# Attention on one core: a step's value products issued ahead of the next pair's score products

## The chip, the cores and the metric

The kernel runs on one core of a Trainium2 chip. The core has a matrix engine (PE; its weight loads are shown as an engine of their own, PEld), a vector engine (DVE), a scalar engine (ACT), a general engine (POOL) and a queue that issues transfers (SP). Each engine works through its own instructions in the order written, and the engines wait for one another through semaphores. The metric is the device time of one execution of the whole program, in microseconds (us).

## The reference

The program is two transformer layers on `x` of 8 batches by 256 rows by 512 columns: a convolution with a gated product, a ternary feed-forward, an attention over `ctx_2048`, and a mixture of experts. The change is in the attention, which is, cut to what is computed:

```python
q = rms_norm(x @ Wq + bq, gq).reshape(b, -1, n, d)          # n = 16 heads of d = 32
k_img = rms_norm(ctx_img @ Wk_img + bk_img, gk_img).reshape(b, -1, n, d)
v_img = (ctx_img @ Wv_img + bv_img).reshape(b, -1, n, d)
scores = jnp.einsum('bqnd,bknd->bnqk', q, k) * scale
probs = jax.nn.softmax(scores, axis=-1)
img_x = jnp.einsum('bnqk,bknd->bqnd', probs, v)
out = (txt_x + img_x).reshape(b, -1, n * d)
return out @ Wo + bo                                        # added to x
```

The image part of the context is its first 257 rows. A batch has 256, so the text part is empty, and each batch attends its 256 queries to its 256 context rows. `x` is layer-normalised before, and the result is layer-normalised again for the experts that follow.

## The kernel before, in words

The attention is one loop (from L1326) over 64 steps plus four iterations that drain the pipeline. A batch has eight steps, k = n % 8: two halves i of 128 query rows, in each two pairs of head groups `cp`, in each two sub-steps p. One step handles four heads for 128 queries, that is 128 x 1024 scores. All engines but SP are held to the order in which the loop writes its instructions (`in_order`, L58), so the source order is the order on PE, DVE, ACT and POOL.

In iteration n these pieces are written, in this order, each for the step that is due:

- `normalise` (L1240) of step n-1: DVE takes the reciprocal `rden` of the row sums, POOL multiplies the probabilities `pr` by it.
- on odd n, `exps` (L1231) of step n: four exponentials on ACT with their row sums.
- on even n, `scores` (L1209) of steps n and n+1: eight products on PE, each on 32 of the array's rows, into two `sc` tiles; then `largest` (L1224) of step n on DVE, which gives `mx`.
- `turn` (L1248) of step n-2: PE transposes `pr` in two groups of four into two `pt` tiles of the tag "tr"; the first is copied to SBUF by DVE (L1262), the second by ACT (L1260). The copies are named `pts`.
- on even n, `largest` of step n+1 and `exps` of step n.
- for k below 6, a piece of the next batch: `middle`, `value` and `end` (L924 to L988) project its k, q and v (eight matmuls of 512 columns, written by `project`, L862), add biases, normalise, and transpose the results. The last batch has no next one, and in the batch before it the value projections come at k = 5 and k = 7 (L1359).
- near the end, normalised rows `dxn` for the experts, which PE transposes into `dxT` (also of the tag "tr") and DVE copies to `xT` (L1312).
- on even n from 4, `values` (L1265) of step n-3: 16 products on PE, each into 32 of the array's columns, which need the four `pts` tiles of steps n-4 and n-3. Their sum `o` is copied by ACT to `oT` (L1278).
- for the last step of each half, `project_out` (L1280): four c-chunks of the output projection into `fo`, which DVE adds to the rows `xs` (L1287) and POOL completes with the bias (L1288). With the halves 0 and 1 of batch 6 it is put off to iterations 56 and 61 (L1318).

The PSUM pool `psC` has two buffers for each tag: "sc" for scores, "tr" for every transposed tile, "mm" for projections, `o` and `fo` alike. A tile takes the buffer of the tile before last of the same tag, and has to wait until that one has been read. In the records every fp32 product of PE shows as two loads and two matmuls.

```python
if 3 <= n < len(steps) + 3 and steps[n - 3].p:
    steps[n - 3].values(steps[n - 4])                 # L1385, L1386
```

Of the kernel before, what the change touches and what calls it, by code (L numbers as in the profile page):

```python
# [78 lines left out]
def tile_kernel(ctx: ExitStack, tc: tile.TileContext, a: dict, out: bass.AP):  # L79
# [795 lines left out]
    def gate_tile(name):  # L875

        pool = experts if len(taken) % 5 == 4 else gates
        taken.append(name)
        return pool.tile([P, DC, TB], F32, tag="gu", bufs=1 if pool is experts else 4, name=name)
# [4 lines left out]
    def gate_weights(names, e, name):  # L884
        gu = gate_tile(f"{name}_gu").rearrange("p c (k f) -> p c k f", k=2)
        for k in range(2):
            nc.sync.dma_start(gu[:, :, k, :], of_expert(names[k], e).rearrange("(c p) f -> p c f", p=P))
        return gu
# [304 lines left out]
    with tc.tile_pool(name="att", bufs=2) as ap_, tc.tile_pool(  # L1193
# [86 lines left out]
        def project_out(b, i, oT):  # L1280
            T = xs[:, i, b, :]
            fo = pc.tile([P, D], F32, tag="mm", name=f"fo{b}{i}")
            for c in range(DC):
                nc.tensor.matmul(  # L1284
                    fo, lhsT=oT[:, c, :], rhs=wsb["Wo"][:, c, :], start=(c == 0), stop=(c == DC - 1)
                )
            nc.vector.tensor_tensor(T, T, fo, ALU.add)  # L1287
            nc.gpsimd.tensor_tensor(T, T, wsb["bo"], ALU.add)  # L1288
# [23 lines left out]
        def turn_in(t, xn):  # L1312
            ps = transposed(pc, xn, f"dxT{t}", "tr")
            nc.vector.tensor_copy(xTs[t // 4][:, :, t % 4 * P : (t % 4 + 1) * P], ps)  # L1314
# [6 lines left out]
        steps, later = [], {}  # L1321
# [4 lines left out]
        for n in range(len(steps) + 4):  # L1326
            coming = None
            k = n % 8
            if n < len(steps):
                if k == 0 and 0 < steps[n][0] < B - 1:  # L1330
                    batches[-1].load()
                if n % 2 == 0:
                    for j in (n, n + 1):
                        steps[j] = Step(batches[steps[j][0]], *steps[j][1:])
                if k < 6 and steps[n].b + 1 < B:
                    coming = batches[steps[n].b + 1]
            if 0 < n <= len(steps):
                steps[n - 1].normalise()
            if coming:
                coming.begin(k)  # L1340
            if n < len(steps) and n % 2:
                steps[n].exps()
            if k == 7 and n > 8:
                finished.root.log()
            if n < len(steps) and n % 2 == 0:
                steps[n].scores(steps[n + 1])
                steps[n].largest()
            if 2 <= n < len(steps) + 2:
                steps[n - 2].turn()
            if n < len(steps) and n % 2 == 0:  # L1350
                steps[n + 1].largest()
                steps[n].exps()
            if coming:
                coming.middle(k)
                if k > 3 and coming.b < B - 1:
                    coming.value(k - 4)
                coming.end(k)
            at = n - (len(steps) - 8)
            if at in (-3, -1):  # L1359
                batches[-1].value((at + 3) // 2)  # L1360
            if at == 1:

                nmr = stat.tile([P, 8], F32, tag="nmr8", bufs=1, name="d_nmr")
                nc.vector.scalar_tensor_tensor(
                    nmr, dmv[:, 0:8, 0], -1.0, dr[:, 0:8], ALU.mult, ALU.mult
                )
            if at == 2:
                for tb in range(2):
                    xTs.append(gate_tile(f"xT{tb}"))
                gu0 = gate_weights(("sg", "sw1"), 0, "s0")  # L1370
            if at in NORMED:
                for t in NORMED[at]:
                    xn = ap_.tile([P, D], F32, tag="xn", bufs=2, name=f"dxn{t}")
                    nc.scalar.activation(
                        xn, xs[:, t % 2, t // 2, :], AF.Identity, bias=nmr[:, t : t + 1], scale=dr[:, t : t + 1]
                    )
                    done_norms[t] = xn
            if k == 7 and n + 9 < len(steps):
                batches.append(Batch((n + 9) // 8, (ap_, ap_), pc))
                batches[-1].moments()  # L1380
            if k == 6 and n > 8:
                finished = Norm((n - 14) // 8)
            elif k == 7 and n > 8:
                finished.factor()
            if 3 <= n < len(steps) + 3 and steps[n - 3].p:  # L1385
                steps[n - 3].values(steps[n - 4])  # L1386
            if n >= 4 and steps[n - 4].cp and steps[n - 4].p:
                s = steps[n - 4]
                if (s.b, s.i) in put_off:
                    later[len(steps) - 8 + put_off[s.b, s.i]] = s  # L1390
                else:
                    project_out(s.b, s.i, s.oT)
            if n in later:
                project_out(later[n].b, later[n].i, later[n].oT)

            for t in NORMED.get(at - 1, ()):
                turn_in(t, done_norms[t])
# [561 lines left out]
```

## Time and profile before

| what | us |
|---|---|
| median of three runs | 1156.17 |
| lowest and highest of them | 1151.67 and 1158.35 |
| the profiled execution's own time | 1151.6 |
| its span, first to last record | 1149.8 |
| first score product of the attention | 380.5 |
| last output projection's add begins | 748.8 |
| one middle batch | 47 |

The profiled execution lies at the low end of the runs, 4.6 us under their median, and 1.8 us of its time lie outside its span. Its granted PE clock is full in all slices.

A line of a timeline is the start in us, the duration in us, the engine, the source line, the operation, the output and inputs, the shapes and the count. What stands in square brackets is the idle time of the engine just before, and what ended it. "issue" means that nothing is shown that it waited for. A line of the stages is the stretch, its length, each engine's busy time with its number of instructions, the clock, the share of the DMA engines and GB/s.

### The profile page before, as it was taken

The page shows a single profiled execution, that of the slowest core. Times are in us where ns is not written, and L with a number is a line of the kernel's source. Part 1 is how long each engine was busy: PE and PEld are TensorE (multiplying, and loading weights), DVE is VectorE, ACT ScalarE, POOL GpSimd, SP SyncE. Part 2 cuts the span into 40 slices and gives each one's busy share as a digit, 9 for nine tenths or more (in the row PEclk, how much of TensorE's full clock was granted, in tenths as well). Part 3 has the DMA queues.
Part 4 walks back from the last instruction along what each step waited for, and adds up shares of the span by engine and source line. Part 5 has one row for each costly group of instructions (what it writes and reads, how often), then busy time and mean ns, then how long its engine had stood idle before and what let it go on. Part 6 is the DMA issues. An engine that isn't in the chain of part 4 may idle for free.

```text
span 1149.8 us, 16488 instructions
## 1 busy us (share of the span) xinstructions
PE 1094.3 (95%) x5866; PEld 658.8 (57%) x5885; DVE 683.6 (59%) x1507; ACT 520.8 (45%) x1173; POOL 440.2 (38%) x501
## 2 busy tenths in 40 slices
PE   4999998899999999999999998899999999999997
PEld 3777775454545555555655555554466766675443
DVE  5998999798866565765656756637612222222452
ACT  4437645798884555656556565531011121111000
POOL 5788887244331243433333434313770000000650
PEclk9999999999999999999999999999999999999999
DMA  7424520699500100000000010052668999997571
GB/s 272 154 74 150 153 76 20 236 305 291 141 1 19 37 1 4 16 19 1 20 20 1 2 38 1 1 194 102 240 202 269 306 338 330 301 314 240 155 248 40
DMA packets 122780, 153.26 MB, mean 133 GB/s; under 512 B 7481, under 2 KB 81273, under 8 KB 122178
## 3 DMA queue, kind: packets, MB, share of 16 engines
q1 hardware_dynamic: 108608, 116.49, 32.1%
q10 hardware_dynamic: 8962, 18.85, 4.6%
q0 software_dynamic: 5120, 16.78, 4.4%
q8 instruction: 49, 0.80, 0.3%
q14 instruction: 41, 0.34, 0.1%
HBM read 107.66 MB, written 44.43 MB: 132 GB/s over the span
## 4 chain that ended last, share of the span: by engine, by line
PE 76%; DVE 14%; POOL 4%; issue 2%; ACT 1%; DMA 1%; SPq 1%; POOLq 0%; DVEq 0%; ACTq 0%
PE r_h L1689 10%; PE gu L1504 9%; PE y L693 5%; PE k_mm L865 5%; PE fo L1284 5%; PE v_mm L865 5%; PE r_po L1705 5%; PE q_mm L865 5%; PE po L1526 5%; PE pt L1255 5%; PE f_op L473 2%; PE sc L1219 2%; PE f_hp L399 2%; PE o L1274 2%; PE o_h L1746 2%
## 5 line engine op out<-in xcount | busy, mean ns | idle before, releaser
L1244 POOL TENSOR_TENSOR pr<-pr,rden 128x1024 f32<-128x1024 f32 x64 | 121.1, 1893 | 155.8 <-DVE rden L1242 140.6
L693 PE MATMUL y<-kv,tp 128*128 128x288 f32 x640 | 161.7, 408 | 5.2 <-DVE wl L716 5.0
L693 PEld LDWEIGHTS y<-kv,tp 128*128 128x128 f32 x640 | 119.0, 190 | 42.5 <-PE y L693 10.1
L1235 ACT ACTIVATE pr<-sc,mx 128x256 f32<-128x256 f32 x256 | 118.3, 483 | 8.1 <-DVE mx L1227 6.9
L1842 POOL DMA_INDIRECT yg<-yd,slot x32 | 33.1, 1035 | 224.4 <-PE gu L1504 206.3
L1689 PE MATMUL r_h<-r_xT,r_gu 128*128 128x256 f32 x512 | 113.7, 380 | 1.5 <-ACT r_xT L1676 1.5
L1689 PEld LDWEIGHTS r_h<-r_xT,r_gu 128*128 128x128 f32 x512 | 96.8, 190 | 22.4 <-issue 8.0
L1227 DVE TENSOR_REDUCE mx<-sc 128x4 f32<-128x1024 f32 x64 | 77.5, 1212 | 4.5 <-PE sc L1219 4.5
L1255 PE MATMUL pt<-ident,pr 128*128 128x128 f32 x512 | 70.6, 279 | 7.5 <-DVE xT L1314 3.5
L1696 DVE SCALAR_TENSOR_TENSOR r_y<-r_h,eb,r_ge 128x256 f32<-128x256 f32 x32 | 15.5, 483 | 97.7 <-PE r_h L1689 94.4
L1260 ACT COPY pts<-pt 128x512 f32<-128x512 f32 x64 | 37.8, 590 | 73.2 <-PE pt L1255 73.2
L1255 PEld LDWEIGHTS pt<-ident,pr 128*128 128x128 f32 x512 | 55.0, 140 | 26.1 <-issue 14.6
L1695 ACT ACTIVATE r_ge<-r_h,gb 128x256 f32<-128x256 f32 x32 | 15.1, 473 | 109.0 <-PE r_h L1689 109.0
L399 PE MATMUL f_hp<-w1q,f_xq 128*128 128x512 bf16 x245 | 59.4, 379 | 5.3 <-ACT f_xq L376 4.5
L631 POOL TENSOR_TENSOR kv<-kx 128x2048 f32<-128x2048 f32 x16 | 57.6, 3601 | 12.9 <-ACT kx L617 12.9
L865 PE MATMUL k_mm<-Wk_sb,cx 128*128 128x512 f32 x128 | 58.1, 598 | 0.0
L865 PE MATMUL v_mm<-Wv_sb,cx 128*128 128x512 f32 x128 | 57.7, 593 | 0.0
L1705 PE MATMUL r_po<-r_w,r_y 128*128 128x512 f32 x128 | 57.7, 593 | 0.0
L1284 PE MATMUL fo<-Wo_sb,oT 128*128 128x512 f32 x128 | 57.7, 593 | 0.0
L865 PE MATMUL q_mm<-Wq_sb,xT 128*128 128x512 f32 x128 | 57.6, 593 | 0.0
L1516 ACT ACTIVATE ge<-gu,gb 128x512 f32<-128x512 f32 x16 | 11.0, 687 | 102.6 <-PE gu L1504 93.8
L473 PE MATMUL f_op<-w2q,f_hq 128*128 128x512 bf16 x249 | 57.0, 379 | 0.4
(486 smaller groups left out, 2104.5 us busy)
## 6 DMA issues: line engine op xcount, KB each, us to landing
xd<-blank SPq DMA_DIRECT2D x1, 15360.0 KB, 59.2
tp<-kpd SPq DMA_DIRECT2D x32, 256.0 KB, 3.3
r_gu<-in_rg SPq DMA_DIRECT2D x16, 512.0 KB, 6.6
r_gu<-in_rw SPq DMA_DIRECT2D x16, 512.0 KB, 6.8
r_w<-in_rw SPq DMA_DIRECT2D x16, 512.0 KB, 6.8
r_xr<-xd SPq DMA_DIRECT2D x16, 512.0 KB, 6.9
yd<-r_yo ACTq DMA_DIRECT2D x32, 256.0 KB, 5.7
yd<-blank SPq DMA_DIRECT2D x1, 6144.0 KB, 77.9
```

The source lines that it names most:

```text
L399: nc.tensor.matmul(dst, lhsT=self.xq[:, i, c, :], rhs=w1q[:, c, cols], start=(c == 0), stop=False)
L473: nc.tensor.matmul(op, lhsT=self.hq[i][:, c, :], rhs=w2q[:, c, :], start=(c == 0), stop=(c == FC - 1))
L693: nc.tensor.matmul(y[:, ll, :, 0:PAIRS], lhsT=tp[:, dl : dl + P], rhs=view(kv, (m0 * G + hh) * PAIRS, [[G * PAIRS, B], [1, PAIRS]]), start ...
L865: nc.tensor.matmul(t, lhsT=lT[:, c, i * P : (i + 1) * P], rhs=w[:, c, :], start=(c == 0), stop=(c == DC - 1),)
L1227: nc.vector.tensor_reduce(self.mx, self.sc.rearrange("p r c k -> p (r c) k"), AX.X, ALU.max, negate=True)
L1235: nc.scalar.activation(self.pr[:, h // 2, h % 2, :], self.sc[:, h // 2, h % 2, :], AF.Exp, bias=self.mx[:, h : h + 1], accum_out=self.den[ ...
L1244: nc.gpsimd.tensor_tensor(flat, flat, rden.unsqueeze(2).to_broadcast([P, 4, S]), ALU.mult)
L1255: nc.tensor.transpose(pt[:, cc, k, :], self.pr[:, rr, cc, k * P : (k + 1) * P], ident)
L1284: nc.tensor.matmul(fo, lhsT=oT[:, c, :], rhs=wsb["Wo"][:, c, :], start=(c == 0), stop=(c == DC - 1))
L1504: nc.tensor.matmul(ps, lhsT=w[0][:, c, k, f * P : (f + 1) * P], rhs=xTs[tb][:, c, :], start=(c == 0), stop=(c == DC - 1),)
L1689: nc.tensor.matmul(ps, lhsT=self.w[0][:, c, k, f * P : (f + 1) * P], rhs=self.xT[:, c, 0:n], start=(c == 0), stop=(c == DC - 1),)
L1705: nc.tensor.matmul(po, lhsT=self.y[:, f, i * P : (i + 1) * P], rhs=self.w[1][:, f, :], start=(f == 0), stop=(f == EC - 1),)
```

## The change

The two lines that write `values` are moved up in the iteration: behind `exps` and the logarithm of the norm, ahead of the scores. Nothing is added or taken away.

```diff
@@ -1342,6 +1342,9 @@
                 steps[n].exps()
             if k == 7 and n > 8:
                 finished.root.log()
+            if 3 <= n < len(steps) + 3 and steps[n - 3].p:
+
+                steps[n - 3].values(steps[n - 4])
             if n < len(steps) and n % 2 == 0:
                 steps[n].scores(steps[n + 1])
                 steps[n].largest()
@@ -1382,8 +1385,6 @@
                 finished = Norm((n - 14) // 8)
             elif k == 7 and n > 8:
                 finished.factor()
-            if 3 <= n < len(steps) + 3 and steps[n - 3].p:
-                steps[n - 3].values(steps[n - 4])
             if n >= 4 and steps[n - 4].cp and steps[n - 4].p:
                 s = steps[n - 4]
                 if (s.b, s.i) in put_off:
```

`values` runs on even n only, since n-3 has to be a step with p = 1. So PE's order in an even iteration goes from scores, transposes, next batch's piece, values to values, scores, transposes, next batch's piece. On ACT the copy to `oT` goes from the iteration's end to a place ahead of the copy of `pts` and of the exponentials.

## The prediction

> **What bounds the kernel now.** I read the page first, then the stages of the attention, then the timeline of one middle batch, its weight loads alone, and the last batch.
>
> ```profile
> PE 1094.3 (95%) x5866; PEld 658.8 (57%) x5885; DVE 683.6 (59%) x1507; ACT 520.8 (45%) x1173; POOL 440.2 (38%) x501
> ...
> PE 76%; DVE 14%; POOL 4%; issue 2%; ACT 1%; DMA 1%; SPq 1%; POOLq 0%; DVEq 0%; ACTq 0%
> ```
>
> PE is the bound, and most of the chain that ended last is PE. The attention divides in two, as the stages show:
>
> ```profile
> core 0: us, PE busy (x) PEld busy (x) DVE busy (x) ACT busy (x) POOL busy (x), PEclk, DMA share, GB/s
> ...
> 568.00:615.00 47.00, 46.86 (x346) 27.06 (x345) 30.18 (x70) 27.59 (x96) 17.60 (x10) 1.00 0.04 12
> ...
> 701.00:749.00 48.00, 41.00 (x401) 26.03 (x400) 28.89 (x56) 28.63 (x91) 21.40 (x14) 1.00 0.01 1
> ```
>
> In a middle batch PE is never idle for long: only what PE's queue itself takes, and any new wait, can move the time. In the last batch, which has no next batch to project, PE idles 7 us and waits in turn for POOL, ACT and DVE; there the order of the small blocks decides.
>
> The timeline of iterations 6 and 7 of a middle batch has the place that matters most:
>
> ```profile
> 553.09 0.74 PEld L1219 LDWEIGHTS sc<-kT_T,qT_T 32*128 32x128 f32 x16 [0.17 <-issue]
> ...
> 554.16 0.86 PEld L1255 LDWEIGHTS pt<-ident,pr 128*128 128x128 f32 x8 [0.33 <-issue]
> ...
> 554.27 1.22 DVE L1227 TENSOR_REDUCE mx<-sc 128x4 f32<-128x1024 f32 x1
> ...
> 555.19 0.81 PEld L1274 LDWEIGHTS o<-pts,v 128*32 128x32 f32 x32 [0.17 <-issue]
> ...
> 555.30 0.59 ACT L1260 COPY pts<-pt 128x512 f32<-128x512 f32 x1 [4.72 <-PE pt L1255]
> 555.41 0.68 DVE L1262 COPY pts<-pt 128x512 f32<-128x512 f32 x1
> ...
> 556.41 0.85 PEld L1255 LDWEIGHTS pt<-ident,pr 128*128 128x128 f32 x8 [0.41 <-POOL pr L1244]
> ```
>
> Here values stand between two transposes of probabilities (554.16 and 556.41), with no projection near. While PE does values, DVE takes the maximum and copies the first `pt`, ACT copies the second: both "tr" buffers are free (556.09, 555.89) before the next transposes.
>
> **The change part by part.** It moves 32 calls. Each issues 16 products on PE (32 loads and 32 matmuls in the records) and one `oT` copy on ACT (0.37 us); nothing on DVE, POOL or SP, and no DMA. PE's calls are moved past eight score products, eight transposes and the next batch's piece, ACT's copy past the `pts` copy, the exponentials and the squares. So PE's work is unchanged; what changes is gaps between blocks, buffers, and when the scores come.
>
> *Gaps.* From load to load, values take 1.01 us (531.43 to 532.44), scores 1.07, transposes 0.82, and a projection with the transposes behind it 4.31, read where the loop has no values yet:
>
> ```profile
> 391.44 0.30 PEld L865 LDWEIGHTS q_mm<-Wq_sb,xT 128*128 128x128 f32 x2
> ...
> 394.55 0.14 PEld L1255 LDWEIGHTS pt<-ident,pr 128*128 128x128 f32 x1 [0.24 <-issue]
> 394.98 0.80 PEld L1255 LDWEIGHTS pt<-ident,pr 128*128 128x128 f32 x7 [0.29 <-issue]
> 395.75 0.30 PEld L865 LDWEIGHTS q_mm<-Wq_sb,xT 128*128 128x128 f32 x2
> ```
>
> The transposes' first load goes ahead of the projection's end; that of values does not. The timeline blames a DVE result for it:
>
> ```profile
> 531.43 0.81 PEld L1274 LDWEIGHTS o<-pts,v 128*32 128x32 f32 x32 [0.76 <-DVE k_r L143]
> ```
>
> Yet scores behind a projection have the same 0.76 us put down to issue (541.21), so this is the projection draining, and no wait that the move removes. In iterations 2 and 3 of a batch the stretch from scores to the second q projection is now 525.89 to 533.27 = 7.38; in the new order it is 1.01 + 1.07 + 0.82 + 4.31 = 7.21, a gain of 0.17. In 4 and 5 it is 7.37 (541.21 to 548.58), a gain of 0.16. In 0 and 1 it is 7.57 (560.87 to 568.44), a gain of 0.36, because a buffer wait goes too:
>
> ```profile
> 568.44 0.30 PEld L865 LDWEIGHTS k_mm<-Wk_sb,cx 128*128 128x128 f32 x2 [0.17 <-DVE k_pre L962]
> ```
>
> The "mm" buffers alternate; with `o` now ahead of the first k projection, the second takes `o`'s buffer, which ACT frees early, and no longer that of the first. Sum: 6 x 0.36 + 6 x 0.17 + 6 x 0.16 = 4.1 us less.
>
> The gap from values to scores is in no row. By what goes out, values leave 0.20 ahead of anything, transposes 0.17, scores 0.33, a projection 0.76. Bounds: 0.17 and 0.76. I take 0.20, since the gap follows what goes out wherever I can compare, and keep 0.33 for the range.
>
> [...]
>
> *The stall between iterations 6 and 7.* In the new order: values 553.09, scores 554.10, transposes 555.17. The maximum follows the scores by 1.18 (541.21 to 542.39), so it runs at 555.28, the `pts` copy of DVE 1.14 behind it at 556.42 to 557.10, and the next transposes, which need that buffer, load 0.06 later at 557.16: 0.75 later than 556.41. POOL's `pr` (to 556.35) is then not the last. Batches 0 to 5: 6 x 0.75 = 4.5 us more.
>
> Is anything else late? DVE is busy without a pause from 554.13 to 569, so it stays 1.01 late until iteration 1, where it waits 3.13 us (572.18); all of it ends there. On the way ACT's copy of the second `pts` of step 5 moves from 560.23 to 560.98 and ends at 561.54, and values of iteration 0 come at 561.62: met by 0.08, and each 0.1 us by which it fails costs 0.6 over six batches. The k projection of iteration 0 now takes `fo`'s buffer, free at 563.96, and comes at 564.5. POOL ends `pr` of step 7 at 567.16, ahead of the transposes at 567.7. I charge nothing for the later scores in iterations 0, 2 and 4 (0.5 to 1.0 us): the 3.6 us projections hide the maximum and the copies. Without that cover it would be another 0.75 each, 18 x 0.75 = 13.5. The `oT` copy costs nothing either: ACT waits there for transposes anyhow (4.72 at 555.30, 3.34 at 543.42); uncovered it is 32 x 0.37 = 12.
>
> [...]
>
> *Batches 6 and 7.* Batch 6 has no projection in iteration 4, so the stall comes there too: its transposes, at 686.39 for POOL, come at 686.41, but DVE's and ACT's later copies are 1.01 and 0.76 late, and the transposes behind them (688.76, 689.59) are held by just these: +0.77 at 689.98. In 6 and 7, +0.95 (696.73 becomes 698.45): +1.72 at the start of batch 7. There I follow the same rules from block to block. These rows of before carry it:
>
> ```profile
> 717.45 0.64 ACT L1260 COPY pts<-pt 128x512 f32<-128x512 f32 x1
> ...
> 717.67 0.73 PEld L1219 LDWEIGHTS sc<-kT_T,qT_T 32*128 32x128 f32 x12 [1.34 <-ACT pr L1235]
> ...
> 722.20 0.42 PEld L1255 LDWEIGHTS pt<-ident,pr 128*128 128x128 f32 x4 [0.58 <-DVE xT L1314]
> ```
>
> ```profile
> 732.82 0.42 PEld L1255 LDWEIGHTS pt<-ident,pr 128*128 128x128 f32 x4 [2.13 <-DVE xT L1314]
> ```
>
> Iteration 58: values wait for the copies of step 55 and push the scores, but the transposes wait for POOL as before: 711.97 becomes 713.48, +1.51. Iteration 60: values need the `pts` of step 57, which ACT copies behind the exponentials at 717.45; with scores behind values, the transposes go from 718.73 to 721.45, +2.72. Iteration 61: DVE's maxima are later, `xT` with them, and 722.20 becomes 725.27, +3.07. Iteration 63: scores behind values cost 1.0 again, and 732.82 becomes 736.89, +4.07. In 64 and 65 a little returns: the last transposes' second half, 741.94 before, comes 3.9 late, and so does all behind it. Batches 6 (from iteration 4) and 7: 3.9 us more. Between +1.7 (batch 7 costs nothing more) and +6 (each of its four scores a full 1.07 late).
>
> Sum: -4.1 + 4.5 + 3.9 = +4.3 us. The profiled execution's 1151.6 becomes 1155.9; against the median of 1156.17, 4.6 above it, 1160.5.
>
> **The rivals.** The forecast is a small loss, below the 0.5% (5.8 us) that a measurement of this kernel can tell from no change.
>
> *Slower: the switch from values to scores costs more.* They split the array in different ways, and no row shows one behind the other. At scores' 0.33 the 30 places give 30 x 0.13 = 3.9 more: +8.2, 1164.4. At 0.76 it is +21, 1177. It decides from 0.25. For it: no row excludes it. Against it: the gap follows what goes out.
>
> *Nothing.* If the last batch gives its 2.2 us back in the routing that follows, or the stall is 0.4, the sum is +2: 1158. The chain of waits, PE in most of its pieces from there on, speaks against it.
>
> *Faster.* If neither stall nor tail appears, the gaps remain: -4.1, 1152.1. It would need `pts` copied ahead of the maximum, which the held order forbids.
>
> **How the numbers follow.** The forecast 0.55, its own range +1 to +8 (a quarter of it beyond 5.8); the switch 0.25; nothing 0.14; faster 0.06. From these: slower 0.55 x 0.25 + 0.25 x 0.9 = 0.36, faster 0.04 (only with the runs' own spread), same 0.60. The range goes from 1155, below the case of nothing by the spread of medians, to 1167, above the switch at 0.33.
>
> **What would show it.** Right: in a middle batch, the second transposes of iteration 7 wait 0.9 to 1.2 us for DVE's `pts`, the wait on `k_pre` is gone, batches take 47.0 to 47.1, and the attention's end moves by about 4. Wrong: a gap above 0.25 ahead of scores behind values; values of iteration 0 waiting for ACT's copy; transposes in iterations 1, 3 or 5 waiting for anything.

## The result, and the profile after

The median went from 1152.82 us (8 runs, 1151.36 to 1158.35) to 1161.97 us (8 runs, 1160.89 to 1164.80): a ratio of 1.0074, 95% interval 1.0054 to 1.0093. That is slower, by more than the 0.5% that tells from no change, where the forecast had put no change first. 1161.97 lies inside the range, 1.5 above the 1160.5.

The times of before fall into groups, for a reason shown below, and 1152.82 lies in the gap between two of them (four of its runs up to 1151.79, four from 1153.84). A median jumps there, so for sums I use means. With the later comparisons there are 58 runs of before, mean 1154.4 (median 1155.13); the 8 runs after have the mean 1162.4. So the change costs 8.0 us, where +4.3 was forecast.

The page's first and fourth parts for the kernel after:

```profile
PE 1096.1 (95%) x5885; PEld 662.6 (57%) x5885; DVE 684.0 (59%) x1507; ACT 522.0 (45%) x1173; POOL 440.5 (38%) x501
...
PE 77%; DVE 15%; POOL 3%; issue 2%; DMA 1%; ACT 1%; SPq 1%; ACTq 0%; DVEq 0%; POOLq 0%
```

PE is the bound as before. The profiled execution took 1160.89 us with a span of 1159.2, against 1151.6 and 1149.8: 9.4 more span. To find where they arise I lined up the first PE load of the same blocks in both traces. The attention starts 0.25 us earlier in the trace after (380.27 against 380.52), and the table has what is added from there to each place. The last column is the prediction's own path, and the column before it is of an experiment told below, in which PE's clock stayed full through the attention.

| block | before | after, later by | same order, clock kept full | predicted |
|---|---|---|---|---|
| iteration 52, first block | 682.34 | +1.18 | +1.18 | +0.36 |
| iteration 54 | 693.61 | +4.75 | +1.93 | +1.13 |
| iteration 56 | 701.19 | +5.76 | +2.93 | +2.08 |
| iteration 60, transposes | 718.73 | +6.79 | +3.96 | +3.08 |
| iteration 63, second half | 732.82 | +8.04 | +5.21 | +4.43 |
| last output projection | 745.07 | +9.64 | +5.12 | +4.3 |

Six batches together bring only 1.18. The large jumps are +3.57 between iterations 52 and 54 and +1.60 behind iteration 63. In the column with the full clock the path is the predicted one, 0.8 higher, all of which is there by iteration 52. The last line counts what lies between the two starts; the span, which grew by 9.4, has the 0.25 in it. That output projection before, after, and in the experiment with the full clock, whose attention starts at 382.57:

```profile
745.07 0.30 PEld L1284 LDWEIGHTS fo<-Wo_sb,oT 128*128 128x128 f32 x2
...
754.46 0.30 PEld L1284 LDWEIGHTS fo<-Wo_sb,oT 128*128 128x128 f32 x2
...
752.23 0.30 PEld L1286 LDWEIGHTS fo<-Wo_sb,oT 128*128 128x128 f32 x2
```

**The middle batch.** The timeline of iterations 6 and 7 after, from one batch's seam to the next:

```profile
553.36 0.81 PEld L1274 LDWEIGHTS o<-pts,v 128*32 128x32 f32 x32 [0.17 <-issue]
554.37 0.74 PEld L1219 LDWEIGHTS sc<-kT_T,qT_T 32*128 32x128 f32 x16 [0.20 <-issue]
554.74 1.89 POOL L1244 TENSOR_TENSOR pr<-pr,rden 128x1024 f32<-128x1024 f32 x1 [3.61 <-DVE rden L1242]
555.45 0.86 PEld L1255 LDWEIGHTS pt<-ident,pr 128*128 128x128 f32 x8 [0.33 <-issue]
555.56 1.22 DVE L1227 TENSOR_REDUCE mx<-sc 128x4 f32<-128x1024 f32 x1 [0.98 <-PE sc L1219]
...
556.70 0.68 DVE L1262 COPY pts<-pt 128x512 f32<-128x512 f32 x1
557.49 0.85 PEld L1255 LDWEIGHTS pt<-ident,pr 128*128 128x128 f32 x8 [1.19 <-POOL pr L1244]
557.52 1.06 PE L1255 MATMUL pt<-ident,pr 128*128 128x128 f32 x8 [0.98 <-DVE pts L1262]
...
561.95 0.81 PEld L1274 LDWEIGHTS o<-pts,v 128*32 128x32 f32 x32 [0.76 <-issue]
...
569.17 0.30 PEld L865 LDWEIGHTS k_mm<-Wk_sb,cx 128*128 128x128 f32 x2
```

The predicted stall is there, 1.19 us. Its line of the weight load names POOL, but POOL's `pr` had ended at 556.63. The matmul's line names the copy `pts`, 556.70 to 557.38, and the loads follow that by 0.11. So the copy that stands behind DVE's maximum is what ended last, as forecast, and the lesson is to read both lines of a PE block. The gap from values to scores is 0.20. The values at 561.95 find `pts` just ready (ACT ended it at 561.82). The second k projection at 569.17 has no wait on `k_pre` any more. Before, a batch took 47.05 us (506.04 to 553.09), now 47.21 (507.16 to 554.37), a little above the 47.0 to 47.1 that the prediction named as a sign.

**The clock.** The stages after, in the same columns as before; the clock is the third number from the end:

```profile
521.00:568.00 47.00, 46.02 (x345) 27.20 (x344) 30.01 (x69) 27.70 (x96) 17.59 (x10) 1.00 0.04 12
662.00:701.00 39.00, 35.81 (x258) 21.37 (x257) 18.81 (x43) 19.14 (x65) 12.53 (x7) 0.91 0.09 28
701.00:740.00 39.00, 30.84 (x299) 19.54 (x297) 25.52 (x49) 26.81 (x94) 17.57 (x11) 1.00 0.00 1
740.00:745.00 5.00, 4.39 (x10) 2.10 (x11) 2.82 (x8) 2.89 (x10) 1.89 (x1) 0.66 0.02 3
```

Before, the stretches of the last two batches show 1.00. After, 0.91 and 0.66. In pieces of half a microsecond the clock is 0.50 from about 689.9 to 696.7 and from 741.1 to 744.5. The first of these places before, at full clock:

```profile
686.39 0.85 PEld L1255 LDWEIGHTS pt<-ident,pr 128*128 128x128 f32 x8 [1.14 <-POOL pr L1244]
688.76 0.42 PEld L162 LDWEIGHTS qT_tr<-ident,q_pre 128*128 128x128 f32 x4 [1.52 <-DVE pts L1262]
...
690.52 0.19 PEld L865 LDWEIGHTS v_mm<-Wv_sb,cx 128*128 128x128 f32 x1 [0.24 <-issue]
```

PE's weight loads after, around both:

```profile
687.40 0.86 PEld L1255 LDWEIGHTS pt<-ident,pr 128*128 128x128 f32 x8 [1.19 <-POOL pr L1244]
690.71 1.57 PEld L162 LDWEIGHTS qT_tr<-ident,q_pre 128*128 128x128 f32 x8 [2.45 <-DVE pts L1262]
...
693.33 0.34 PEld L865 LDWEIGHTS v_mm<-Wv_sb,cx 128*128 128x128 f32 x1 [0.52 <-issue]
...
697.16 0.19 PEld L865 LDWEIGHTS v_mm<-Wv_sb,cx 128*128 128x128 f32 x1 [0.24 <-issue]
...
740.61 0.42 PEld L1255 LDWEIGHTS pt<-ident,pr 128*128 128x128 f32 x4 [2.62 <-DVE xT L1314]
...
741.97 0.34 PEld L1284 LDWEIGHTS fo<-Wo_sb,oT 128*128 128x128 f32 x1 [0.52 <-issue]
```

Behind each of the two longest idle times a projection's loads come 0.85 apart (0.34 + 0.52) and not 0.43 (0.19 + 0.24): half speed, until 696.7 in the first case. The jumps of the table are these two places. Against the column with the full clock they come to 9.64 - 5.12 = 4.5 us.

The two drops last 6.8 and 3.4 us at 0.50. No gap of the weight loads in the attention after is longer than 2.62 us.

All 8 runs after have a mean clock between 0.989 and 0.995. Of the 50 runs of before in the later comparisons, 18 have 0.998 or 0.999 (1151.1 to 1152.4 us, median 1151.6), 28 have 0.995 or 0.996 (1153.9 to 1156.7) and 4 have 0.991 (1158.3 to 1158.8). So before loses clock too in most of its runs, just not in the one that was profiled. On the mean it loses 1154.4 - 1151.6 = 2.8 us by it.

### The profile page after: what moved, and what is told of

Its sections match the earlier page's. It is cut to its first block, busy times and chain, and to the rows that moved or that the text cites. A ratio compares the mean times of both kernels' runs of the same rounds, so it can differ in the third digit from the quotient of the medians.

```text
span 1159.2 us, 16506 instructions
## 1 busy us (share of the span) xinstructions
PE 1096.1 (95%) x5885; PEld 662.6 (57%) x5885; DVE 684.0 (59%) x1507; ACT 522.0 (45%) x1173; POOL 440.5 (38%) x501
## 4 chain that ended last, share of the span: by engine, by line
PE 77%; DVE 15%; POOL 3%; issue 2%; DMA 1%; ACT 1%; SPq 1%; ACTq 0%; DVEq 0%; POOLq 0%
PE r_h L1690 10%; PE gu L1505 9%; PE y L693 5%; PE v_mm L865 5%; PE fo L1284 5%; PE k_mm L865 5%; PE r_po L1706 5%; PE q_mm L865 5%; PE po L1527 5%; PE pt L1255 4%; PE sc L1219 3%; PE o L1274 3%; PE f_op L473 2%; PE f_hp L399 2%; PE o_h L1747 2%
```

## The experiments

The theory after the result: the order alone costs about 5 us at full clock (of the parts that were forecast), and the longer waits of the last two batches let PE's clock drop, which costs the rest. The rivals: one of the three parts is mis-sized by the whole difference (projection places that gain nothing, or a stall that is dearer), and the clock is an accident of the one profile. Three runs do one part of the change alone, one changes the stall, four fill PE's idle times.

**1. Only the 18 places behind a projection** (iterations 0, 2 and 4 of a batch, up to iteration 50):

```diff
+            early = k in (0, 2, 4) and n < 52
-            if 3 <= n < len(steps) + 3 and steps[n - 3].p:
+            if early and 3 <= n < len(steps) + 3 and steps[n - 3].p:
                 steps[n - 3].values(steps[n - 4])
...
+            if not early and 3 <= n < len(steps) + 3 and steps[n - 3].p:
+                steps[n - 3].values(steps[n - 4])
```

> Values ahead of the scores only in iterations 0, 2 and 4 of a batch up to iteration 50, where a projection follows; elsewhere behind, as before. Theory (the loss comes from iteration 6 and from iteration 52 on, and the gaps are a gain): 18 places gain 0.16 to 0.36 us each, 4.1 in all, the wait on k_pre is gone, and the time is 1152.8 - 4.1 = 1148.7, ratio 0.9965. Rival (late scores cost something in every iteration): no gain or a loss, ratio 1.000 or above.

Measured: 1151.47 (12 runs) against 1155.74 (22 runs), ratio 0.9970 [0.9954, 0.9986]. It is faster by 0.3%, with an interval that stays below 1. At full clock one run took 1147.8, against 1151.6 for before: 3.8 less. In the traces iteration 54 comes 3.66 sooner. The 18 places do bring the forecast gain, a little short of 4.1. The wait on `k_pre`, which carries half of the gain in iterations 0 and 1, wasn't there in batch 1, so the places gain 5 x 0.34 + 0.15, and iterations 2 to 5 gain 12 x 0.15: 3.65 in all.

This trace of the experiment keeps the order of before in the last batch, with the waits of before (2.13 ahead of the second half in iteration 63), and its clock dropped there nevertheless, twice, at 716 to 719 (eight transposes load in 1.57 us, where the same eight take 0.86 elsewhere) and 733 to 736 (a projection's loads come 0.85 apart); the mean of the stretch is 0.91:

```profile
701.00:740.00 39.00, 32.66 (x292) 20.34 (x290) 23.53 (x43) 25.27 (x85) 18.65 (x12) 0.91 0.00 1
```

These two drops take back 3.3 of the 3.65: the last output projection comes only 0.37 sooner. A third drop, at 197 to 200, lies in the convolution (0.87 on the mean from 190 to 203, where before has 1.00).

**2. Only iteration 6 of batches 0 to 5:** as 1, with

```diff
+            early = k == 6 and n < 52
```

> Values ahead only in iteration 6 of batches 0 to 5, elsewhere behind. Theory: each of the six batches has its second transposes wait for DVE's copy of the first, 0.75 to 0.8 us more each, 4.5 to 4.9 in all, time 1157.5. Rival (the stall at that place is taken up by a later wait of the same batch): below 1 us in all.

Measured: 1160.65 (5 runs), ratio 1.0057 [1.0033, 1.0081]. The traces add 5.89 us up to iteration 52, about 1.0 a batch. The stall takes 0.81 of it. The rest is at the start of the next batch, where values still stand at the old place and wait longer for the `k_pre` of the first projection. The timeline of the weight loads in this run:

```profile
572.12 0.30 PEld L865 LDWEIGHTS k_mm<-Wk_sb,cx 128*128 128x128 f32 x2 [0.37 <-DVE k_pre L962]
```

0.37 where before has 0.17. The expectation took over the 0.75 and missed this. It is not a part of the whole change, in which that wait is gone. Behind iteration 52 this trace too has the order of before, and its clock dropped there twice, at 724 to 727 (eight transposes load in 1.57 us) and 741 to 744 (a projection's loads come 0.85 apart); that is in the times, and not in the 5.89.

**3. Only from iteration 52 on:** as 1, with

```diff
+            early = n >= 52
```

> Values ahead only from iteration 52 on. Theory (two costs at the end: later scores, and PE idle long enough that its clock is halved twice): waits 4 to 5 us and the clock 4.5, time 1161 to 1162.5, mean granted clock 0.995 or lower. Rival (the clock fell in the changed kernel because of the middle batches or by chance): clock 0.999 as before, and only the 4 to 5 us of waits, time 1157.

Measured: 1160.13 (7 runs), ratio 1.0054 [1.0035, 1.0073]. Five runs at a mean clock of 0.995 took 1159.3 to 1160.5, two at 0.990 took 1162.1 and 1162.2. The attention's end moves by 7.24 us, where 3.9 was forecast for the order, and the attention has two drops of the clock, at 691 to 694 and 722 to 725 (0.96 on the mean from 662 to 701 and from 701 to 740). An estimate from the mean clocks leaves some 1.6 us for other places: 0.995 over a span of 1157.5 us is 5.8 us of clock, the two stretches of 39 us at 0.96 hold 3.1 of them, and 1.1 is what before's 0.999 stands for. The rounding of the clocks can move it by as much. No run of it kept the full clock.

The traces without fillers tell the two batches apart. The wait ahead of the q transposes in iteration 53 is 2.45 us in the changed order, and the clock drops there in all three traces that have it (after, 3 and 4). It is 1.52 in the order of before, and the clock drops there in none of the three (before, 1 and 2). In the last batch the clock drops with either order: twice in 1 and in 2, not at all in before. So a drop that the change brings shows in batch 6; in the last batch it is left open how much the longer waits add.

By the means, against the 1154.4 of before, the three parts are -3.1, +6.4 and +6.1. Less the 1.0 that the second has for itself (5.89 - 6 x 0.81) they sum to +8.4, close to the +8.0 of the whole. The means have the lost clock in them. Against the forecast -4.1, +4.5 and +3.9 the parts lack 1.0, 0.9 and 2.2, so no part holds the whole difference, and the last lacks most.

**4. The stall, with DVE and ACT exchanged.** In iteration 6 ACT copies the first `pt`, which DVE's maximum no longer holds up, and DVE the second:

```diff
-            def turn(self):
+            def turn(self, swap=False):
...
-                    if rr:
+                    if bool(rr) != swap:
                         nc.scalar.copy(pts, pt)
...
-                steps[n - 2].turn()
+                steps[n - 2].turn(k == 6 and n < 52)
```

> The changed kernel, with the two copies of the transposes in iteration 6 of batches 0 to 5 exchanged: ACT, which idles there, empties the first tile and DVE, which has the maximum first, the second. Nothing else moves. Theory (DVE's place behind the late scores holds the first buffer): the second transposes no longer wait 1.2 us; their first half starts about 0.7 earlier, their second half waits for DVE, and the next block starts 0.4 to 0.5 earlier, 2.4 to 3 us over six batches. Rival (POOL's product of the probabilities holds them, as the list of waits names it): they start when POOL is done, at most 0.8 earlier in the first half, and also the second half does; 4 to 5 us over six batches. Second rival (the order on PE holds them): nothing changes.

The lines of the timeline:

```profile
556.07 0.86 PEld L1255 LDWEIGHTS pt<-ident,pr 128*128 128x128 f32 x8 [0.33 <-issue]
556.77 0.59 ACT L1260 COPY pts<-pt 128x512 f32<-128x512 f32 x1 [1.26 <-PE pt L1255]
557.32 0.68 DVE L1262 COPY pts<-pt 128x512 f32<-128x512 f32 x1
557.47 0.42 PEld L1255 LDWEIGHTS pt<-ident,pr 128*128 128x128 f32 x4 [0.54 <-POOL pr L1244]
...
558.05 0.42 PEld L1255 LDWEIGHTS pt<-ident,pr 128*128 128x128 f32 x4 [0.17 <-DVE pts L1262]
```

The first four transposes of iteration 7 come 1.40 us behind those of iteration 6, not 2.04, and their wait falls from 1.19 to 0.54. Only the copying engines were exchanged, so the copy that waits for DVE's maximum is what the stall is. Not all of the 0.64 is kept, because values of iteration 0 now wait for ACT: its copy runs to 562.24, and these values load from 562.07 in 1.01 us where they need 0.81. By iteration 52 this order is 1.57 ahead of the change as it was, 0.26 a batch, where 2.4 to 3 were expected. Median 1160.35 (7 runs), ratio 1.0048 [1.0032, 1.0064], against 1.0074: the intervals overlap, so the traces carry this verdict, not the times.

**5. Filling two idle times with unread transposes** (iterations 53 and 61), on the change as it was:

```diff
+        def busy(count):
+            idle = pc.tile([P, DC, P], F32, tag="mm", name=f"idle{n}_{count}")
+            for j in range(count):
+                nc.tensor.transpose(idle[:, j % DC, :], ident, ident)
...
+            if n in (53, 61):
+                busy(6)
             if 2 <= n < len(steps) + 2:
                 steps[n - 2].turn()
+            if n in (53, 61):
+                busy(14)
```

> The changed kernel, with 6 and 14 transposes of a constant that nobody reads in the idle stretches of PE in iterations 53 and 61, 40 in all, 0.6 and 1.5 us long, shorter than the waits there. Theory (idle PE is what halves the clock): the granted clock stays at 0.999, the two slow stretches are gone, time 1162 - 4.5 = 1157.5. Rival (the drop has another cause, or the waits are the whole loss): clock 0.995 or lower, time 1162 or more.

The stages around both places:

```profile
686.00:700.00 14.00, 12.01 (x110) 8.48 (x109) 9.11 (x18) 6.33 (x23) 5.31 (x3) 1.00 0.01 1
738.00:746.00 8.00, 6.45 (x12) 3.27 (x13) 3.70 (x11) 3.94 (x13) 1.89 (x1) 0.57 0.00 0
```

Where the filler met the wait, the clock stayed at 1.00 and the stretch from the q transposes to the values fell from 7.40 to 4.57 us. At the other place I had the wrong iteration: the long wait stands in 63, not 61. There the filler only delayed PE (5.69 to 7.21 us from the `dxT` transposes to the next values), the wait of 2.62 stayed, and the clock fell. Median 1161.83 (5 runs), ratio 1.0064 [1.0043, 1.0086]: inconclusive as a whole, and repeated as 6.

**6. Filling the waits of the last two batches, at the right places.** 66 transposes (the expectation says 63). They stand ahead of values, ahead of `turn`, between its two halves (the argument of `turn`), behind it, and ahead of `dxT`:

```diff
+            if n in {60: 10}:
+                busy({60: 10}[n])
...
+            if n in {53: 6, 55: 6}:
+                busy({53: 6, 55: 6}[n])
...
-                steps[n - 2].turn()
+                steps[n - 2].turn({63: 14}.get(n, 0))
+            if n in {53: 14}:
+                busy({53: 14}[n])
...
+            if n in {58: 4, 60: 6, 62: 6}:
+                busy({58: 4, 60: 6, 62: 6}[n])
```

> The changed kernel, with transposes of a constant that nobody reads in nearly all idle stretches of PE from iteration 53 to 63 (63 transposes, at most 14 in one place, each group shorter than the wait that it fills). Theory (idle PE halves the clock, and at full clock the move costs 4.9): mean clock 0.997 to 0.999 in nearly all runs, 1156 to 1157.5. Rival (the clock falls for another reason): 0.992 as in the changed kernel, 1162 or more.

The stages from iteration 52 on:

```profile
662.00:701.00 39.00, 37.99 (x288) 23.47 (x287) 21.51 (x48) 21.64 (x74) 14.75 (x9) 1.00 0.09 28
701.00:740.00 39.00, 34.94 (x340) 23.89 (x338) 25.53 (x49) 27.15 (x97) 17.52 (x10) 1.00 0.01 1
740.00:745.00 5.00, 4.92 (x33) 2.79 (x37) 3.08 (x10) 2.71 (x9) 1.92 (x2) 1.00 0.00 0
```

Median 1158.04 (10 runs, 1156.7 to 1158.7), ratio 1.0023 [1.0007, 1.0039] to the before of its own comparison, where the change had 1.0074 [1.0054, 1.0093]. Every one of the 10 runs is below the lowest of the change as it was, 1160.89. More work on PE made the program some 4 us faster, and the clock in the attention is full; the mean clock of the ten runs is 0.996 to 0.999, where the change as it was had 0.989 to 0.995. So the clock is no accident of the profile: in the last two batches the idle time causes the drops, and filling it removes them (1.00 in the three stretches above, where the change as it was has 0.91, 1.00 and 0.66). One drop is left, to 0.50 at 198 to 202, in the convolution (besides one to 0.50 in the last 4 us, such as before's trace too has in its last 2.4). The four runs at 0.998 and 0.999 took 1156.7 to 1157.0, median 1156.9, against 1151.6 for before at that clock: the order alone costs 5.2 us, and the table's column, taken from this trace, says +5.12. Of that, 5.12 - 1.18 = 3.94 arise from iteration 52 on, where 3.9 was forecast.

**7. A version of both.** The order of 1, which gains, with fillers in the last batches (iterations 53, 58 and 63):

```diff
+            early = k in (0, 2, 4) and n < 52
...
+            if n in {53: 6, 58: 14}:
+                busy({53: 6, 58: 14}[n])
...
-                steps[n - 2].turn()
+                steps[n - 2].turn({63: 12}.get(n, 0))
+            if n in {53: 8}:
+                busy({53: 8}[n])
```

> Values ahead in iterations 0, 2 and 4 up to 50, behind elsewhere, and transposes that nobody reads in four idle stretches of PE in iterations 53, 58 and 63 (40 in all). Theory: the gaps' gain at full clock, 1151.5 - 4.1 = 1147.4, in most runs, against a median of 1155.7 of the kernel before, ratio 0.993. Rival (filling does nothing for the clock): as without it, 1151.5, ratio 0.997.

Measured: 1149.95 (8 runs, 1147.9 to 1151.1), ratio 0.9961 [0.9945, 0.9977]. It beats both kernels, the one before by 0.4%. Two runs at 0.999 took 1147.9 and 1148.3; the profile of another has drops at 198 to 201 and, behind a wait of iteration 60 that has no filler (1.34 us), at 716 to 720, both to 0.50. Against 1 (0.9970) the fillers' share isn't resolved.

**8. The fillers alone, on the order of before:**

```diff
+            if n in {53: 6, 58: 14}:
+                busy({53: 6, 58: 14}[n])
...
-                steps[n - 2].turn()
+                steps[n - 2].turn({63: 12}.get(n, 0))
+            if n in {53: 8}:
+                busy({53: 8}[n])
```

> The kernel before, with the same 40 transposes. Theory: its runs at 1155.8 (clock 0.995) and 1158.4 (0.991) are those in which idle PE halved the clock in the last batch, so nearly all runs come to 1151.5 at 0.999. Rival: the three groups of times remain, median 1155.7.

Measured: 1154.17 (12 runs), ratio 0.9992 [0.9978, 1.0005]: no difference that shows. Four runs at 0.999 took 1151.2 to 1151.7 and eight at 0.994 to 0.996 took 1154.0 to 1155.0. The expectation was that the second group would vanish, and it did not. In the profiled run of the second group the attention is at full clock, and the drops lie elsewhere, in the convolution:

```profile
190.00:203.00 13.00, 9.18 (x37) 5.69 (x39) 10.75 (x32) 3.96 (x7) 9.11 (x29) 0.74 0.05 7
225.00:231.00 6.00, 4.13 (x13) 1.35 (x14) 3.98 (x10) 4.55 (x6) 1.48 (x5) 0.72 1.10 358
```

That theory is half met: with the fillers this run keeps the attention's clock, but the group near 0.995 stays. Its attention starts 2.40 us later than in the trace of before and is then as long, to 0.02 us, so the fillers themselves cost nothing, and what this run lost it lost ahead of the attention. The trace of before has waits of 1.79 at 197.0 and 2.41 at 224.3 too, and kept its clock there. What makes an execution lose it at 196 or 226 us, where nothing was changed, stays open.

## Why the prediction was right or wrong, point by point

- **The gaps, -4.1 in 18 places: right, 0.45 too large.** They brought 3.65. Iterations 2 to 5 gained 0.15 a place (forecast 0.17 and 0.16); iterations 0 and 1 gained 0.34, except 0.15 in batch 1, where the buffer wait wasn't there.
- **The gap from values to scores, 0.20: right.** 0.20 at all 30 places. The rival of the switch falls. The reason given for it, "the gap follows what goes out", is half of what these traces show: that holds where the tile shape of the loads changes. Behind transposes a projection, which has the same 128x128 shape, loads with no gap at all (56 places after), values and scores after 0.17; behind a projection transposes load after 0.24, values and scores after 0.76.
- **The stall, 6 x 0.75: right in place and cause, a little small.** The wait came at 1.19 (0.9 to 1.2 forecast), for the copy behind the maximum; it costs 0.81 a batch, 6 x 0.06 = 0.36 more. "Met by 0.08" for the values of iteration 0 was met by 0.13. Transposes in iterations 1, 3 and 5 of batches 0 to 5 wait for nothing, as forecast.
- **The last two batches, +3.9: right for the order.** +3.94 at full clock, block by block along the table.
- **The sum, +4.3: 0.9 too small at full clock.** +5.1 by the trace, +5.2 by the runs; the 0.45 of the gaps and the 0.36 of the stall make up the difference.
- **The step that failed** is the one that isn't in the sum. "In the last batch, which has no next batch to project, PE idles 7 us" was read as time in which the order of small blocks decides, and every duration behind it was taken at the clock of the one profile. The change lengthened two waits of the last two batches, from 1.52 to 2.45 us and from 2.13 to 2.62, and in the trace after PE ran at half speed (0.50) behind them for 6.8 and 3.4 us: 4.5 us. That the lengthening did it is borne out for the first by the traces (all three with 2.45 dropped, none of the three with 1.52); behind the second the clock also fell with the 2.13 of before (runs 1 and 2). By the runs, after loses 1162.4 - 1156.9 = 5.5 us to the clock on the mean, where before loses 2.8: 2.7 more. With the order's 5.2 this is the 8.0. Both losses can hold drops in the convolution, as runs 1, 6, 7 and 8 show them, so how much of the 2.7 lies in the attention isn't measured apart. No term of the sum stood for it, and no rival either, so no change was taken as likeliest, where the measurement shows slower.
- **The offset hid it.** The median of three and the profiled run stood 4.6 apart, and the prediction added the 4.6 as a constant. It was a cost of the same kind, lost clock: runs of before at 0.995 or 0.996 take 1153.9 to 1156.7. Where they lose it no trace of before shows; the traced run of 8, the same order with fillers, lost it in the convolution. That a profile at full clock stood so far below the median was the sign that most runs of this program lose clock somewhere. As a constant it made the time come out close (1160.5 against 1161.97), which was luck, since the change itself was put at about half.
- **The other rivals.** "Nothing" (the tail given back) falls: the last output projection is 9.64 late and the span grew by 9.4. "Faster" falls with the stall.

## What to carry to other kernels

Where PE is the bound, price the idle times twice: what they last, and what PE's clock does behind them; here the drops behind two waits of 2.5 and 2.6 us cost 2.8 and 1.7 us in the projections that follow. When the profiled run lies some us below the median of the runs, look for the clock before calling it spread, since one profile can be the execution in which nothing dropped. And a move that gains at one kind of place and loses at another should be made only there: the 18 places behind a projection alone beat both kernels' order, before's by 0.3%.

## What the runs showed of the hardware that was not expected

- PE's clock went to 0.50 at idle times shorter than the drops: gaps of 1.19 and 2.45 us within 4.5 us (686.21 to 690.71) went with 6.8 us, and 2.62 us with 3.4 us. After the same idle times it fell in some executions and not in others: the last batch in the order of before (2.12 to 2.13 us idle in iteration 63) kept 1.00 in the trace of before and lost clock twice in those of 1 and 2.
- 66 transposes on PE that nobody reads, in time in which it would have idled, made the changed order about 4 us faster.
- Most of the drop in iteration 53 was paid in the projection behind it: from the first v load to the next block 5.85 us at half clock (after), 3.63 at full (before), 2.22 of the 2.8 us.
- The gap ahead of a block on PE depends on both neighbours: where no other engine is waited for, none to 0.24 us between blocks of the same 128x128 shape, 0.17 to 0.76 us where the shape changes (all PE blocks of the attention, before and after).
- A weight load and the matmul behind it can name different releasers for one wait. The load named POOL, which had been done for 0.86 us; the matmul named the DVE copy that ended it.
